# Stores off SyncE's queue, the last stage's first tile prepared during the second binary convolution, sums of y taken with VectorE's additions

## The chip, the cores and the metric

The kernel runs on one core of a Trainium2 chip. A core has five engines that run side by side, each with its own instruction stream in a fixed order: TensorE (PE, matrix products; PEld is its loading of weights), VectorE (DVE), ScalarE (ACT), GpSimd (POOL) and SyncE (SP, which here only starts DMA transfers). Any of ACT, POOL and SP can start a DMA; a transfer that waits for its data holds up what stands behind it in the same engine's stream. An engine waits for another by a semaphore. Data that is worked on lies in SBUF (128 partitions); PE writes to PSUM. The metric is the device time in microseconds (us).

## The reference

A tensor `x` of shape (4, 256, 64, 64), float32, goes through four residual layers, each `x = x + layer(group_norm(x))` with 32 groups of 8 channels. Layer 0 is an axial attention, layer 1 a 3x3 convolution with ternary weights, layer 2 a binary block and layer 3 a 3x3 convolution with a full set of weights. The change touches layers 1 to 3. Layer 2, cut to what matters (its input is the group norm of x):

```python
x = channel_shuffle(x, 2)
xa, xb = jnp.split(x, 2, axis=1)                      # 128 channels each
x1 = leaky_relu(gconv3x3(jnp.sign(x), w1, groups=2))  # 256 -> 128 channels
x2 = batchnorm_train(x1, g1, b1)                      # over batch and image
x3 = channel_shuffle(batchnorm_train(jnp.concatenate((x2 + xa, xb), 1), g2, b2), 2)
x4 = batchnorm_train(leaky_relu(gconv3x3(jnp.sign(x3), w2, groups=2)), g3, b3)
x5a, x5b = jnp.split(x3, 2, axis=1)
return jnp.concatenate((x4 + x5a, x5b), axis=1)
```

`batchnorm_train` needs mean and variance over all four images, so nothing after it can use its scale before the last image's convolution is through. Layer 3 needs, for each image, the group norm of `x + layer 2`, with statistics for each image and group of 8 channels. Of the 256 channels that layer 2 returns, the first 128 hold x4 and the other 128 (x5b) don't: for those, layer 3's input can be made without the last batch norm (the kernel's tile t = 1).

## The kernel before

The layers run as stages one after the other; after the attention (to about 1521 us of the profiled execution) come stage "d" (layer 1), the binary block "e" (layer 2) and stage "g" (layer 3). A scheduler puts the instructions of each engine into one fixed order by priority, mostly that of the program; `tc.high_priority()` raises what stands in it. Each stage's SBUF tiles come from pools laid one after another; the pools of the next stage lie over those of the one before, so a tile can be filled as soon as the old tile under it is done with.

*Stages "d" and "g"* share `conv_layer`. The channels are two halves t = 0 and 1 of 128. An image half tile (t, h) holds 32 rows. The convolution is made with a row transform: `input_rows` makes of the padded tile `pad` six combinations of rows (12 DVE operations, lines 970 to 986, result `dtr` or `gtr`), `output_rows` multiplies each of the six with three shifted weights for both t (36 products of 128x512, float32, each two records in the trace, line 998) and combines the six sums on ACT and DVE (lines 1016 to 1033) and adds them to x. That is one chunk (b, h, co): 4 images x 2 halves x 2 halves of output channels = 16 chunks. For the first chunk, products of one t are all issued ahead of those of the other (`order`, which is (1, 0) in stage g). `prepare(b, t)` loads a tile, adds up x and takes its statistics; `norm` gets group means with small matmuls (`pst`, lines 111 to 122) and rsqrt (ACT, line 102); `transform` writes the normalised tile into the pad (ACT, lines 1108 and 1112) and calls `input_rows`. `rest` interleaves the chunks of an image with `prepare`, `norm` and `transform` of the next. Results are stored by `finish_1` (`x2_d`, line 1184) and `finish_3` (`out`, line 1484), on SP. In the names of the trace digits are left out: `x_d` is `x2_d`, `u_d` is `u3_d`.

*Stage "e"* has two binary convolutions, each of 16 chunks (4 images, 4 quarters q) of 72 bf16 matmul records (line 1230). `prepare_1` loads x2 (line 1311), writes signs into `e_pad` (ACT, line 1322), and `binary_rows` makes `e_tr` (DVE, line 1220). `binary_conv` copies one of the four sums (ACT, line 1238), combines them (DVE, 1239 to 1242), applies the leaky relu (DVE, two additions of 512 columns, line 1245: the result is y, which stays in SBUF), and takes on ACT the sum (1247) and the sum of squares (1248) of y. `chunk_1` also takes the sum of y times x (DVE 1334 into `junk`, ACT 1337). After convolution 1 the statistics of the whole batch give scales. `prepare_2` scales x (ACT 1427), adds y (DVE 1431), stores the result z on SP (`z_d`, 1434) and takes its signs (ACT 1440). `chunk_2` overwrites y with the second convolution's result and stores it on SP after every second chunk (`y_d`, 1449). `sums_affine` (1285) turns the sums of the batch into the last batch norm's scale `sy2` and shift `cy2`.

*Stage "g"* then starts: it zeroes its pads on POOL, loads six weight tiles of 768 KB on SP (1068), and for t = 1 and then 0 prepares image 0. `load_3` loads 1 MB halves of x (1461), then in eighths of a tile parts of z and x2 (1468, 1469), added by DVE (1470), and for t = 0 y (`yq`, loaded at 1475, added at 1476 with scale `sy2`); the statistics are DVE's (1037). In program order all of this stands behind the second binary convolution and its sums. These lines set the order of stage g's start:

```python
        set_up()
        load_weights()
        for t in (1, 0):
            prepare(0, t)
            norm(0, slice(t, t + 1))
            transform(0, t, 0)
        for t in (1, 0):
            transform(0, t, 1)
        rest()
```

## Time and profile before

| | us |
|---|---|
| median of 3 runs | 2985.82 |
| lowest and highest | 2976.44, 2987.91 |
| the profiled execution's own time | 2981.28 |
| its span | 2979.5 |
| stage d, where PE is busy 480.43 of 481 | 1618 to 2099 |
| binary convolution 1 | 2105 to 2242 |
| statistics | 2242 to 2267.3 |
| binary convolution 2 | 2267.3 to 2415.5 |
| first matmul of stage g's convolution | 2460.76 |
| last one ends, about | 2971.4 |

Read it by stages: the busy shares of the whole span mix stages with different limits. From 2494 to the end of its matmuls stage g keeps PE busy without a gap, as stage d does; the idle stretches of PE lie at the borders of the binary block. The granted TensorE clock is 0.940 of full speed over the span and about 1.00 in stage g's convolution once it runs.

### The profile page before, as it was taken

The page shows a single profiled execution, that of the slowest core. Times are in us where ns is not written, and L with a number is a line of the kernel's source. Part 1 is how long each engine was busy: PE and PEld are TensorE (multiplying, and loading weights), DVE is VectorE, ACT ScalarE, POOL GpSimd, SP SyncE. Part 2 cuts the span into 40 slices and gives each one's busy share as a digit, 9 for nine tenths or more (in the row PEclk, how much of TensorE's full clock was granted, in tenths as well). Part 3 has the DMA queues.
Part 4 walks back from the last instruction along what each step waited for, and adds up shares of the span by engine and source line. Part 5 has one row for each costly group of instructions (what it writes and reads, how often), then busy time and mean ns, then how long its engine had stood idle before and what let it go on. Part 6 is the DMA issues. An engine that isn't in the chain of part 4 may idle for free. (4 is left out here: it accounts for less than half of the span.)

```text
span 2979.5 us, 77554 instructions
## 1 busy us (share of the span) xinstructions
PE 2605.9 (87%) x34248; PEld 1609.6 (54%) x34248; DVE 2066.4 (69%) x3555; ACT 1084.8 (36%) x2073; POOL 55.7 (2%) x119
## 2 busy tenths in 40 slices
PE   7999889899999778888845999999996848999998
PEld 4656556677767566667642444444453533444443
DVE  6555997666666466666667898884777859869553
ACT  4554444555545644555401011011468620101100
POOL 0000000000000100000000000000000000000000
PEclk9999999999999798999867999999997978999999
DMA  6867465555464777888654533413336544243201
GB/s 234 265 202 216 133 189 140 139 142 138 111 143 109 224 254 242 266 264 269 218 180 165 181 112 120 161 51 146 104 120 228 210 180 136 95 147 109 92 28 43
DMA packets 246807, 484.65 MB, mean 163 GB/s; under 512 B 28672, under 2 KB 128640, under 8 KB 220608
## 3 DMA queue, kind: packets, MB, share of 16 engines
q1 hardware_dynamic: 190080, 349.19, 35.1%
q10 hardware_dynamic: 53728, 117.46, 14.3%
q0 software_dynamic: 2656, 12.98, 1.2%
q8 instruction: 271, 4.44, 0.6%
q14 instruction: 72, 0.59, 0.1%
HBM read 283.20 MB, written 196.35 MB: 161 GB/s over the span
## 5 line engine op out<-in xcount | busy, mean ns | idle before, releaser
L998 PE MATMUL gc<-gtr,g_u 128*128 128x512 f32 x1152 | 501.3, 597 | 21.4 <-issue 13.0
L998 PE MATMUL dc<-dtr,d_u 128*128 128x512 f32 x1152 | 503.6, 598 | 17.1 <-DVE dtr L984 11.6
L478 DVE STREAM_TRANSPOSE t<-pd 128x1024 f32<-128x1024 f32 x256 | 304.1, 1227 | 114.7 <-PE pd L471 114.7
L998 PEld LDWEIGHTS gc<-gtr,g_u 128*128 128x128 f32 x1152 | 218.6, 191 | 296.3 <-issue 283.6
L998 PEld LDWEIGHTS dc<-dtr,d_u 128*128 128x128 f32 x1152 | 217.8, 191 | 288.8 <-issue 265.4
L471 PE MATMUL pd<-rm,qb 64*32 64x256 f32 x8192 | 285.0, 388 | 51.9 <-DVE t L478 42.7
L490 PEld LDWEIGHTS pq<-t,t 64*64 64x64 f32 x8192 | 261.7, 137 | 72.0 <-issue 46.9
L1230 PE MATMUL pc<-e_tr,e_k 128*64 128x512 bf16 x2304 | 266.1, 392 | 39.0 <-ACT pc_o L1238 20.2
L490 PE MATMUL pq<-t,t 64*64 64x64 f32 x8192 | 281.3, 221 | 16.1 <-issue 14.0
L494 ACT ACTIVATE o<-pq 128x512 f32<-128x512 f32 x256 | 152.4, 595 | 321.9 <-PE pq L490 321.9
L1230 PEld LDWEIGHTS <-e_k 128*64 128x64 bf16 x2304 | 154.2, 112 | 149.6 <-issue 51.0
L797 ACT ACTIVATE pt<-pt,sm 128x512 f32<-128x512 f32 x256 | 162.9, 709 | 188.5 <-DVE pt L767 151.6
L471 PEld LDWEIGHTS pd<-rm,qb 64*32 64x32 f32 x8192 | 156.4, 108 | 135.0 <-DVE t L478 59.9
L767 DVE TENSOR_TENSOR pt<-e_False,si_False 128x1024 f32<-128x1024 f32 x128 | 151.5, 1218 | 41.0 <-PE e_False L757 40.8
L499 ACT ACTIVATE pq<-pq 128x512 f32<-128x512 f32 x256 | 149.8, 585 | 3.9
L757 PE MATMUL e_False<-qc_False,rw 32*128 32x256 f32 x1024 | 126.3, 478 | 20.8 <-DVE pt L767 11.7
L1016 ACT COPY gc_c<-gc 128x512 f32<-128x512 f32 x32 | 18.6, 581 | 343.7 <-PE gc L998 343.7
L1016 ACT COPY dc_c<-dc 128x512 f32<-128x512 f32 x32 | 18.7, 584 | 329.0 <-PE dc L998 329.0
L279 PE MATMUL po<-xg,wt 128*128 128x512 f32 x256 | 123.6, 623 | 9.2 <-DVE st L286 7.6
L835 PE MATMUL pa_False<-pt,vb 128*32 128x64 f32 x4096 | 100.9, 239 | 28.5 <-issue 18.0
L859 PE MATMUL pe_False<-pt,ve 128*32 128x64 f32 x4096 | 92.1, 245 | 32.6 <-issue 24.5
L294 PE MATMUL pv<-wt,xg 128*128 128x256 f32 x512 | 120.6, 384 | 0.0
(383 smaller groups left out, 3406.1 us busy)
## 6 DMA issues: line engine op xcount, KB each, us to landing
si_False<-qk_d SPq DMA_DIRECT2D x64, 1024.0 KB
qk_d<-o ACTq DMA_DIRECT2D x124, 512.0 KB
x<-x_d SPq DMA_DIRECT2D x32, 1056.0 KB
a<-at_d SPq DMA_DIRECT2D x256, 128.0 KB
xa<-in_x SPq DMA_DIRECT2D x16, 1024.0 KB
vt_d<-vs ACTq DMA_DIRECT2D x32, 512.0 KB
q_d<-qs SPq DMA_DIRECT2D x64, 256.0 KB
qb<-q_d SPq DMA_DIRECT2D x128, 128.0 KB
```

The source lines that it names most:

```text
L279: nc.tensor.matmul(psf, lhsT=wt[:, t, bass.ts(o, P)], rhs=xg[:, t, :], start=(t == 0), stop=(t == 1))
L294: nc.tensor.matmul(pv[:, j, :], lhsT=xg[:, t, pix], rhs=wt[:, t, C : 2 * C], start=(t == 0), stop=(t == 1),)
L471: nc.tensor.matmul(pds[t][32 * c : 32 * c + 32, m].rearrange("p j k -> p (j k)"), lhsT=q[rows, 2 * (gp % 2) + g, a, 32 * nb : 32 * nb + 32 ...
L478: nc.vector.transpose(ts[t][:, :, 32 * jh : 32 * jh + 32].rearrange("p a j b -> p j a b"), pds[t].rearrange("p m j k -> p j m k"),)
L490: nc.tensor.matmul(ps[rows, m, :], lhsT=ts[1][rows, n // 2, :, n % 2], rhs=ts[0][rows, n // 2, :, n % 2], start=True, stop=True, tile_posi ...
L494: nc.scalar.activation(o[:, :, 8 * k : 8 * k + 8, :], ps.rearrange("p n (a b) -> p a n b", b=2), AF.Copy, accum_out=acc[:, 0, gp, col : co ...
L499: nc.scalar.activation(psf, psf, AF.Square, accum_out=acc[:, 1, gp, col : col + 1])
L757: nc.tensor.matmul(es[x_ // 2][:, x_ % 2, :, :, par], lhsT=rw[rows, 63 - i : 127 - i].rearrange("p j r -> p (j r)"), rhs=q[rows, :, par, k ...
L767: nc.vector.tensor_tensor(dst, e, src, ALU.add)
L797: nc.scalar.activation(s, s, AF.Exp, scale=s2q[:, gp : gp + 1])
L998: nc.tensor.matmul(ms[k], lhsT=u[:, t, dx, k, bass.ts(co, P)], rhs=vs[t][:, k, :, dx : dx + 64], start=(first and dx == 0), stop=(last and ...
L1230: nc.tensor.matmul(m[64 * g : 64 * g + 64], lhsT=parts[:, g, i, k, dx, :], rhs=vs[g][:, k, 8 * (q % 2) : 8 * (q % 2) + 8, dx : dx + 64], s ...
```

## The change

Five things are changed.

1. The stores of x2, z and out go from SP's queue to GpSimd's, those of y to ACT's. Stage g's weights are loaded on GpSimd's queue, in the order t = 1, then t = 0. The pads of "d" and "g" are zeroed on DVE.
2. The sum of y (line 1247) and that of y times x (1337) are no longer taken by ACT: the DVE operations that make y and `junk` carry an accumulating output (`accum_out`); the product with x becomes a `scalar_tensor_tensor`. ACT keeps the squares.
3. `prepare(0, 1)`, `norm` and `transform` of image 0's tile t = 1 are no longer behind the second binary convolution: they have a higher priority, and the pools of "e" and "g" are laid in another order, so that the tiles they need don't lie over tiles that are still in use. In the resulting order on DVE their operations stand among those of the second convolution's last nine chunks, and five of the eight additions of z and x2 for t = 0 stand there too. On PE the 18 products of t = 1 for the first chunk follow the last binary matmul directly, and the group means of t = 0 come after them.
4. For image 0 and t = 0 alone the statistics are made of sums: the addition of y on DVE has an accumulating output, and ACT squares the result with another; the squares are written over the `yq` tile, of which there are two.
5. `transform(0, t, 1)` is pinned to its place in program order. In the resulting order on DVE, 15 additions and statistics for image 1 stand between t = 0's additions and the end of its 12 transform rows.

The core of the diff (bookkeeping of arguments is left out):

```diff
-    def input_rows(v, pad):
+    def input_rows(v, pad, pinned):
...
         stt = nc.vector.scalar_tensor_tensor
-        stt(v[:, 5], d[2], -4.0, d[4], ALU.mult, ALU.add)
+        start = stt(v[:, 5], d[2], -4.0, d[4], ALU.mult, ALU.add)
+        if pinned:
+            tc.keep_in_program_order(start)
         stt(v[:, 0], d[1], -4.0, d[3], ALU.mult, ALU.add)
...
         xslots = {k: pool(ph, f"{name}_x{k}") for k in x_order}
+        if name == "g":
+            op = pool(ph, f"{name}_o", 2)
         wp = pool(ph, f"{name}_w")
-        op = pool(ph, f"{name}_o", 2)
+        if name == "d":
+            op = pool(ph, f"{name}_o", 2)
         tslots = {k: pool(ph, f"{name}_t{k}") for k in tr_order}
...
         def set_up():
             for h in range(2):
-                nc.gpsimd.memset(pads[h][:, 33 * h, :], 0.0)
-                nc.gpsimd.memset(pads[h][:, 1 - h : 34 - h, 0], 0.0)
-                nc.gpsimd.memset(pads[h][:, 1 - h : 34 - h, 65], 0.0)
-
-        def load_weights():
-            for t in first:
-                for dx in range(3):
-                    nc.sync.dma_start(out=u[:, t, dx], in_=weights[:, t, dx])
+                nc.vector.memset(pads[h][:, 33 * h, :], 0.0)
+                nc.vector.memset(pads[h][:, 1 - h : 34 - h, 0], 0.0)
+                nc.vector.memset(pads[h][:, 1 - h : 34 - h, 65], 0.0)
+        def load_weights(t, eng):
+            for dx in range(3):
+                eng.dma_start(out=u[:, t, dx], in_=weights[:, t, dx])
...
             st = sp.tile([P, NB, 6], F32, name=f"{name}st_{b}_{t}", tag=f"st{t}")
-            shifts[b, t] = load(b, t, place(b, t), ap_, st, sp, pst)
-            nc.vector.bn_aggr(mvs[b][:, t, :], st.rearrange("p k s -> p (k s)"))
+            shifts[b, t], done = load(b, t, place(b, t), ap_, st, mvs[b][:, t, :], sp, pst)
+            if not done:
+                nc.vector.bn_aggr(mvs[b][:, t, :], st.rearrange("p k s -> p (k s)"))
             if shifts[b, t] is not None:
...
-        def transform(b, t, h):
+        def transform(b, t, h, pinned=False):
...
             v = tslots[s].tile([P, 6, 8, 66], F32, name=f"{name}tr_{b}_{t}_{h}", tag="tr")
-            input_rows(v, pads[h])
+            input_rows(v, pads[h], pinned)
             vs[b, t, h] = v
...
             half_stats(st_x2[b, co], h, xh)
-            nc.sync.dma_start(out=x2_d[b][bass.ts(co, P), bass.ts(h, HW // 2)], in_=xh)
+            nc.gpsimd.dma_start(out=x2_d[b][bass.ts(co, P), bass.ts(h, HW // 2)], in_=xh)
             if h == 1:
...
             prepare(0, 0)
-        load_weights()
+        for t in range(2):
+            load_weights(t, nc.sync)
         norm(0, slice(0, 1))
...
-    def binary_conv(psp, lp, parts, vs, q, dst, st, name):
+    def binary_conv(psp, lp, parts, vs, q, dst, sums, squares, name):
...
         for r in range(2):
-            nc.vector.scalar_tensor_tensor(rows[:, r], o[:, r], 0.01, o[:, r], ALU.mult, ALU.max)
-        of = o.rearrange("p r q w -> p (r q w)")
-        nc.scalar.activation(of, dst, AF.Copy, accum_out=st[:, 0:1])
-        nc.scalar.activation(of, dst, AF.Square, accum_out=st[:, 1:2])
+            nc.vector.scalar_tensor_tensor(
+                rows[:, r], o[:, r], 0.01, o[:, r], ALU.mult, ALU.max, accum_out=sums[:, r : r + 1]
+            )
+        nc.scalar.activation(o.rearrange("p r q w -> p (r q w)"), dst, AF.Square, accum_out=squares)
...
         padp = pool(ph, "e_p")
+        jp = pool(ph, "e_j")
+        yp = pool(ph, "e_y")
         sp = pool(ph, "e_s")
-        yp = pool(ph, "e_y")
         lp = pool(ph, "e_l")
         wp2 = pool(ph, "e_w2")
-        tslots = {k: pool(ph, f"e_t{k}") for k in (0, 2, 3)}
+        tslots = {k: pool(ph, f"e_t{k}") for k in range(4)}
         wp1 = pool(ph, "e_w1")
-        tslots.update({k: pool(ph, f"e_t{k}") for k in (1, 4, 5)})
+        tslots.update({k: pool(ph, f"e_t{k}") for k in (4, 5)})
         padq = pool(ph, "e_q")
-        jp = pool(ph, "e_j")
         psb = pool(ph, "e_pst", 1, PSUM)
...
         nmr2 = small(keep, [P, B, 2])
-        st = [sp.tile([P, B, 4, 2], F32, name=f"st_y{i}") for i in range(2)]
-
-        def sums_affine(st, gamma, beta):
+        sums = [sp.tile([P, B, 4, 2], F32, name=f"sum_y{i}") for i in range(2)]
+        squares = [sp.tile([P, B, 4], F32, name=f"sq_y{i}") for i in range(2)]
+        def sums_affine(i, gamma, beta):
             tot = small(sp, [P, 2])
-            nc.vector.tensor_reduce(tot, st.rearrange("p b q k -> p k (b q)"), AX.X, ALU.add)
+            nc.vector.tensor_reduce(tot[:, 0:1], sums[i].rearrange("p b q r -> p (b q r)"), AX.X, ALU.add)
+            nc.vector.tensor_reduce(tot[:, 1:2], squares[i].rearrange("p b q -> p (b q)"), AX.X, ALU.add)
             mv = small(sp, [P, 2])
...
         def chunk_1(b, q, vs):
             dst = y[b][:, bass.ts(q, 1024)]
             junk = jp.tile([P, 1024], F32, name=f"junk_{b}_{q}", tag="junk")
-            nc.vector.tensor_tensor(
-                junk, dst, xa[b, h][:, r : r + 16, :].rearrange("p h w -> p (h w)"), ALU.mult
+            nc.vector.scalar_tensor_tensor(
+                junk, dst, 1.0, xa[b, h][:, r : r + 16, :].rearrange("p h w -> p (h w)"), ALU.mult, ALU.mult,
+                accum_out=cross[:, b, q : q + 1],
             )
-            nc.scalar.activation(junk, junk, AF.Copy, accum_out=cross[:, b, q : q + 1])
...
         my = small(sp, [P, B])
-        nc.vector.tensor_reduce(my, st[0][:, :, :, 0], AX.X, ALU.add)
+        nc.vector.tensor_reduce(my, sums[0].rearrange("p b q r -> p b (q r)"), AX.X, ALU.add)
...
                     )
-                    nc.sync.dma_start(out=z_d[b][:, bass.ts(h, HW // 2)], in_=xf[:, 64 * h : 64 * h + HW // 2])
+                    nc.gpsimd.dma_start(out=z_d[b][:, bass.ts(h, HW // 2)], in_=xf[:, 64 * h : 64 * h + HW // 2])
                 for g in range(2):
...
         def chunk_2(b, q, vs):
...
                 cols = bass.ts(q // 2, HW // 2)
-                nc.sync.dma_start(out=y_d[b][:, cols], in_=y[b][:, cols])
-
-        images(prepare_2, chunk_2, [prepare_2(0, h) for h in range(2)])
-        _, sy2, cy2 = sums_affine(st[1], vec[:, V_G3 : V_G3 + 1], vec[:, V_B3 : V_B3 + 1])
+                nc.scalar.dma_start(out=y_d[b][:, cols], in_=y[b][:, cols])
+        with tc.high_priority():
+            ready = [prepare_2(0, 0)]
+        ready.append(prepare_2(0, 1))
+        images(prepare_2, chunk_2, ready)
+        _, sy2, cy2 = sums_affine(1, vec[:, V_G3 : V_G3 + 1], vec[:, V_B3 : V_B3 + 1])
...
-        def load_3(b, t, xh, ap_, st, sp, pst):
+        def load_3(b, t, xh, ap_, st, mv, sp, pst):
+            first = b == t == 0
             for half in range(2):
...
                         nc.sync.dma_start(out=yq, in_=y_d[b][:, part])
-                        nc.vector.scalar_tensor_tensor(xt[:, cols], yq, sy2, xt[:, cols], ALU.mult, ALU.add)
-                half_stats(st, half, xt)
+                        if not first:
+                            nc.vector.scalar_tensor_tensor(xt[:, cols], yq, sy2, xt[:, cols], ALU.mult, ALU.add)
+                            continue
+                        k = 4 * half + q
+                        nc.vector.scalar_tensor_tensor(
+                            xt[:, cols], yq, sy2, xt[:, cols], ALU.mult, ALU.add, accum_out=st[:, k, 0:1]
+                        )
+                        nc.scalar.activation(yq, xt[:, cols], AF.Square, accum_out=st[:, k, 1:2])
+                if not first:
+                    half_stats(st, half, xt)
             if t == 1:
-                return sg[:, 1, 1, b : b + 1]
+                return sg[:, 1, 1, b : b + 1], False
+            if first:
+                nc.vector.tensor_reduce(mv, st[:, :, 0:2].rearrange("p k s -> p s k"), AX.X, ALU.add)
+                nc.vector.tensor_scalar(mv, mv, 1.0 / HW, None, ALU.mult)
+                m2 = small(sp, [P, 1])
+                nc.vector.tensor_tensor(m2, mv[:, 0:1], mv[:, 0:1], ALU.mult)
+                nc.vector.tensor_tensor(mv[:, 1:2], mv[:, 1:2], m2, ALU.subtract)
+                nc.vector.tensor_scalar(mv[:, 1:2], mv[:, 1:2], 0.0, None, ALU.max)
             nc.vector.tensor_tensor(shift_y[:, b : b + 1], sg[:, 0, 1, b : b + 1], cy2, ALU.add)
-            return shift_y[:, b : b + 1]
+            return shift_y[:, b : b + 1], first
         def finish_3(b, h, co, xh, sp, pst):
-            nc.sync.dma_start(out=out[b, bass.ts(co, P), bass.ts(h, HW // 2)], in_=xh)
+            nc.gpsimd.dma_start(out=out[b, bass.ts(co, P), bass.ts(h, HW // 2)], in_=xh)
         set_up, load_weights, prepare, norm, transform, rest, sp, pst = conv_layer(
-            "g", ph, u3_d, (0, 1, 2, 3, 4, 5), (0, 1, 2, 4, 3, 5), M_GRP, load_3,
+            "g", ph, u3_d, (0, 1, 2, 3, 4, 5), (2, 3, 4, 5, 0, 1), M_GRP, load_3,
             vec[:, V_L3B : V_L3B + 2], (1, 0), finish_3,
         )
-        set_up()
-        load_weights()
+        with tc.high_priority():
+            set_up()
+        prepare(0, 1)
+        load_weights(1, nc.gpsimd)
+        with tc.high_priority():
+            norm(0, slice(1, 2))
+            transform(0, 1, 0)
+        load_weights(0, nc.gpsimd)
+        prepare(0, 0)
+        norm(0, slice(0, 1))
+        transform(0, 0, 0)
         for t in (1, 0):
-            prepare(0, t)
-            norm(0, slice(t, t + 1))
-            transform(0, t, 0)
-        for t in (1, 0):
-            transform(0, t, 1)
+            transform(0, t, 1, True)
         rest()
```

## The prediction

> **What bounds the kernel now.** I read the page first (span, clock), then tables of engine busy time cut at the stage borders, then the chain of waits and the timeline around the borders. Columns of the next fence: stretch in us, its length, then busy time (and instructions) of PE, PEld, DVE, ACT, POOL, then granted PE clock, DMA share, GB/s.
>
> ```profile
> span 2979.5 us, 77554 instructions
> 1618.00:2099.00 481.00, 480.43 (x1138) 212.70 (x1139) 383.56 (x677) 57.43 (x68) 1.81 (x12) 0.99 0.36 121
> 2105.00:2242.00 137.00, 131.20 (x1158) 73.28 (x1158) 112.47 (x190) 86.85 (x117) 0.00 (x0) 0.98 0.38 127
> 2242.00:2267.30 25.30, 1.71 (x11) 1.50 (x10) 19.34 (x57) 17.58 (x20) 0.00 (x0) 0.55 0.31 120
> 2267.30:2345.00 77.70, 63.10 (x500) 35.27 (x502) 61.87 (x86) 76.02 (x58) 0.00 (x0) 0.90 0.68 250
> 2345.00:2415.50 70.50, 70.50 (x642) 45.55 (x639) 51.12 (x81) 30.72 (x51) 0.52 (x6) 0.99 0.41 150
> 2415.50:2494.20 78.70, 28.57 (x76) 13.34 (x72) 58.22 (x128) 12.39 (x15) 0.00 (x0) 0.67 0.57 200
> 2601.00:2971.40 370.40, 370.40 (x872) 163.42 (x871) 227.51 (x384) 33.67 (x42) 0.00 (x0) 1.00 0.23 83
> ```
>
> The ternary convolution (1618 to 2099) and the last stage after 2494 are bound by PE. Binary convolution 1 (2105 to 2242) nearly so. The statistics (2242 to 2267) leave PE idle. Binary convolution 2 is bound by ACT in its first 77.7 us (76.02 busy) and by PE in the rest. From 2415.5 to 2494.2 PE works 28.57 of 78.7 us. That hole is what the change is aimed at; its waits and timeline:
>
> ```profile
> PE pst L111 <- DVE sm L1086: 28.5, 1, 28.5
> PE pc L1230 <- ACT pc_o L1238: 20.2, 9, 4.5
> PE gc L998 <- issue: 13.0, 1, 13.0
> ...
> 2342.92 72.52 PE pc L1230 x648
> 2419.61 4.97 DMA y_d<-y
> 2424.66 13.72 DMA gx<-x_d
> ...
> 2448.91 2.11 ACT g_pad L1108
> ...
> 2460.76 16.80 PE L998 MATMUL gc<-gtr,g_u 128*128 128x512 f32 x32 [13.02 <-issue]
> 2487.43 6.00 PE L998 MATMUL gc<-gtr,g_u 128*128 128x512 f32 x10 [7.58 <-DVE gtr L977]
> ```
>
> After the last binary matmul (T0 = 2415.5) the last y store, the six weight loads and the first gx load go through SP one behind the other; gx is there at 2438.4. Then come its statistics, ACT's pad and DVE's 12 rows of the transform; PE starts the last convolution at 2460.76, 45.3 us after T0. One chunk of it takes 30.9 us (two ACT copies of the same place in neighbouring chunks of the ternary stage, at 2025.41 and 2056.31), 16 chunks 494.4; it ends at 2971.4, after 510.6. So 16.2 us go to a cold start (32 matmuls in 16.8 us where 0.429 each gives 13.7) and the waits up to 2494. The last store ends 8.1 us later.
>
> **The change, part by part.**
>
> *Stores of x2, z and out to GpSimd's queue, y to ACT's, pad memsets to DVE.* In the ternary stage PE is busy 480.43 of 481 us: nothing there moves the end (0; without that cover the 12 memsets are 12 x 0.16 = 2 us). The memsets of e_pad stand on POOL between stores of the ternary stage's last image; the ACT pass that fills the pads last ends 40 us before binary convolution 1, cover for a late one. z and x2 are read back a stage later. The weights (6 x 768 KB) now stand behind z's last store on POOL, about 80 us before T0 (the additions that make z end near 2330 to 2340); at the 5.4 us that a 768 KB load of POOL's queue takes (u_d<-u) even one at a time they are in after 33, if their place in SBUF is free, which no view shows. The eight y stores cost ACT their issue, 0.32 each as on SP: 2.6 us, from ACT time that the sums set free. The `out` stores hide under matmuls, save the last: 5.6 us now; 5.4 x 1024/768 = 7.2 by the POOL row. Term: +1.6, bounds 0 and +3.
>
> *Sums of y.* ACT loses 32 copies with sums (L1247: 1.055 + 0.187) and 16 over junk (L1337: 1.041 + 0.186): 39.7 us in convolution 1 with half of the former, 19.9 in convolution 2. DVE gets them as an accumulator on 64 additions of 512 columns and 16 of 1024: one accumulator read each. The only such addition in the trace is L456: 0.421 for 256 columns, read 0.084. L1245 without accumulator is 0.689 for 512. Both fit 0.155 + 1.04 ns a column, so the accumulator slows L456 by nothing but its read; but L456 has one operand in PSUM, L1245 both in SBUF. I take 0.084 a piece (bounds 0 and, if such an operation ran at half its rate and its read cost ACT's 0.187, 0.72 per 512 columns).
>
> [...]
>
> Convolution 1: 16 chunks x 72 matmuls at 0.1117 (72.52/648 = 0.1119) are 128.7 of 137 us. DVE goes to 112.47 + 48 x 0.084 = 116.5, still below; ACT to 47. Of the 8.3 us above full rate, the waits for ACT's copy L1238 (20.2 us over both convolutions) should go, not those for x. Term -4, bounds -8.3 and 0. Statistics: behind the last y ACT has L1247 (1.24) and L1337 (1.23) less, DVE three reads more: -2.2, bounds -2.5 and 0.
>
> *First tile of the last stage (t=1 of image 0) inside convolution 2.* Counted in the order of instructions: DVE gets in the last nine chunks 13 additions like L1470 (0.75), 8 statistics (0.69), 12 transform rows (0.64 from start to start), 6 memsets and some 15 small ones (0.16), and 18 accumulator reads: 9.8 + 5.5 + 7.7 + 3.4 + 1.5 = 27.9. Second part of convolution 2: DVE 51.1 + 27.9 = 79 in 70.5 us, so DVE becomes its bound: +8.5. First part: seven chunks without L1247 take 8.7 from ACT, which bound it: -8.7 (PE needs 56, DVE 62). Together about 0, bounds -8.7 and +12 (small waits: PE now has this tile's group sums between its matmuls and waits there for DVE, with chunks 15 and 16 queued behind them; ACT's norm and pad stand likewise ahead of the copy of the last chunk; a miss delays both convolutions' PE work by the miss). This tile's loads (two of gx, 16 of x) cost SP some 0.55 each, 10 us, in a stretch where DMA is busy to 0.41, and ACT's 5 us of pads lie where ACT is busy 30.7 of 70.5.
>
> *The hole.* t=1's products, half a chunk (15.5 us), follow T0 at once, PE warm. Then PE waits for t=0. Its chain from T0: output work and y 4.1, ACT's square 1.2, coefficients 2: sy2 at T0 + 7.5 (before: T0 + 9). Eight additions of y: two yq lie ready, and each further pair waits for addition (0.75), ACT's square of it (about 0.85), a load (2.6, the x load at 2439.69) and its turn: some 4.3 us a round, three rounds, so done at T0 + 23. Sums, group means and rsqrt 5 (2445.3 to 2448.9 plus additions), pad 2.1: T0 + 30. The transform shares DVE with additions for image 1 (15 such operations ordered among its 12 rows): its first rows at T0 + 33, all at T0 + 41; before, five such were among its 12 rows. PE takes the first two kinds of product (5.2 us) from T0 + 34 and goes on at T0 + 41, as if it had started at T0 + 36. Remaining 494.4 - 15.5 = 478.9, plus 3 cold: last matmul at T0 + 518 against T0 + 555.9. Term -38; bounds -48 (t=0 ready at T0 + 26, no cold loss) and -22 (t=0 another 16 later, by loads).
>
> Sum: 0 + 1.6 - 4 - 2.2 + 0 - 38 = -42.6. The profiled execution took 2981.28 (span 2979.5 and 1.8 around it): 2938.7. It lies 0.15% below the median 2985.82, within the spread of 11.5; I say 2939.
>
> **The rivals.**
>
> *A, the early tile is paid back.* DVE is in order, and at 79 of 70.5 us has no slack; a tile's load or a wait for PE's sums adds to it in full. Convolution 2 +12, t=0 at its late bound: 1.6 - 4 - 2.2 + 12 - 22 = -14.6: 2967. For it: DVE was 88% busy in the changed half; against: t=1's inputs are ready since convolution 1.
>
> *B, half rate for the accumulating additions* (0.53 per 512 columns): convolution 1 has 64 such pieces: 34 us on DVE's 116.5 make 150, +13 over 137; convolution 2 +17; last stage +4: 1.6 + 13 - 2.2 + 17 - 34 = -5: 2976. For: no row shows two SBUF operands with an accumulator; against: L456 loses nothing.
>
> *C, the slower side.* The same place, but an accumulating addition of two SBUF operands costs e = 0.9 per 512 columns (half rate, a read like ACT's, and its write waited out). DVE has 20 us of slack in convolution 1, none after: 64e - 20 + 32e + 8e over the -38.6 of the other terms; it decides from e = 0.56 on. At 0.9: +35, that is 3016. Only the missing row speaks for it.
>
> *D, better than forecast:* t=0 early and convolution 2 at full rate: about -60: 2921.
>
> **How the numbers follow.** Forecast 0.58, A 0.19, B 0.08, C 0.07, D 0.08. What this kernel's measurement tells from no change is about 0.5%, 15 us. A's 0.19 are split, by its nearness to that bound, into 0.10 faster, 0.07 same and 0.02 slower; B is same, C slower: faster 0.58 + 0.08 + 0.10 = 0.76, same 0.15, slower 0.09. The range: D's end at 2915, and A wholly inside, 2972; B and C are left out.
>
> **What would show it.** L1247 and L1337 gone; the additions at L1252 at 0.69 with reads of 0.08 (B and C: 1.2 or more). Convolution 2 still near 148 us, with DVE over 90% busy in its second half. PE's wait between t=1's and t=0's products about 20 us; first t=0 product at T0 + 34. The forecast is wrong if PE waits again for `g_u`, or if convolution 1 is longer than 137.

## The result, and the profile after

The changed kernel takes 2949.84 us (median of 16 runs, 2937.56 to 2976.9); the kernel before takes 2986.42 on the same chip (16 runs, 2976.44 to 3001.58). The ratio is 0.9884, 95% interval 0.986 to 0.9908: 36.6 us faster, less than the 42.6 forecast. The profiled execution of the changed kernel took 2953.15 us with a span of 2951.4.

The next fence is the table of busy time by stretch of the changed kernel, columns as in the prediction: binary convolution 1, the statistics, convolution 2 in two parts, and two pieces of what was the hole. Line numbers behind the change are higher: L1230 is now L1237, L1238 is L1245, L1245 is L1252, L998 is L1000, L1470 is L1484 and L1476 is L1494; in the experiments they move by a few lines more.

```profile
2111.46:2244.10 132.64, 128.36 (x1160) 68.94 (x1159) 113.61 (x236) 57.62 (x62) 0.53 (x1) 1.00 0.41 140
2244.10:2266.05 21.95, 1.53 (x8) 1.38 (x9) 18.59 (x62) 13.28 (x12) 1.54 (x3) 0.62 0.34 126
2266.05:2336.00 69.95, 68.57 (x596) 36.00 (x598) 64.79 (x108) 68.80 (x49) 2.19 (x5) 0.97 0.78 282
2336.00:2407.20 71.20, 65.42 (x566) 38.71 (x562) 57.36 (x118) 24.51 (x32) 3.74 (x7) 0.95 0.71 259
2407.20:2417.40 10.20, 0.00 (x0) 0.00 (x0) 10.20 (x20) 1.74 (x3) 0.00 (x0) 0.63 0.12 35
2432.80:2456.40 23.60, 7.61 (x14) 3.68 (x14) 15.51 (x42) 6.58 (x15) 0.00 (x0) 0.67 0.61 192
```

Convolution 1 is 4.4 us shorter and the statistics 3.1. Convolution 2 now holds the early tile's work and is still 9 us shorter (150.1 to 141.1). Its first half is filled by ACT (68.80 of 69.95 us busy) and PE (68.57) alike; in the second no engine is full: DVE is 57.36 of 71.20 us busy, where the forecast had it as the bound. Its last matmul ends at 2407.17, which is T0 from here on. (The prediction took 2415.5 as T0 of the kernel before; that kernel's last binary matmul ends at 2417.4. By that T0 its last product ends 554.0 us later, not 555.9.) For the first 10.2 us after T0 PE does nothing at all while DVE is busy throughout, and there is a second gap before the tile t=0. These are PE's waits from convolution 1 to the last stage's start:

```profile
PE pst L111 <- DVE sm L1092: 16.5, 2, 11.5
PE pc L1237 <- DVE e_tr L1227: 14.9, 1, 14.9
PE gc L1000 <- DVE pc_o L1249: 10.2, 1, 10.2
PE psg L1401 <- DVE sg L1403: 5.5, 1, 5.5
PE gc L1000 <- DVE gtr L979: 4.6, 1, 4.6
PE pc L1237 <- ACT pc_o L1245: 2.3, 4, 1.1
```

ACT's copy, which PE waited for longest in convolution 2 before, is nearly gone (2.3 us). The 16.5 us in the first line are two waits of PE's group mean matmuls (`pst`) for the sums that DVE makes for them ("group sums" below), one inside convolution 2, one in the hole. PE's timeline shows both in their places:

```profile
2390.20 0.59 PE L111 MATMUL pst<-sm,mt 128*128 128x1 f32 x2 [5.00 <-DVE sm L1092]
2390.71 1.49 PE L1237 MATMUL pc<-e_tr,e_k 128*64 128x512 bf16 x6
...
2394.69 12.48 PE L1237 MATMUL pc<-e_tr,e_k 128*64 128x512 bf16 x105
2417.40 15.32 PE L1000 MATMUL gc<-gtr,g_u 128*128 128x512 f32 x28 [10.23 <-DVE pc_o L1249]
2444.25 0.59 PE L111 MATMUL pst<-sm,mt 128*128 128x1 f32 x2 [11.53 <-DVE sm L1092]
...
2456.47 3.78 PE L1000 MATMUL gc<-gtr,g_u 128*128 128x512 f32 x4 [4.61 <-DVE gtr L979]
```

PE waits 5.00 us inside convolution 2 for the early tile's own statistics; the six matmuls behind the wait take 1.49 us, 0.25 each instead of 0.112. After T0 the early tile's first product starts 10.2 us late: it waits for DVE's combination of the last chunk (L1249). t=0's first product stands at T0 + 49.3 (2456.47), where the forecast had T0 + 34 (32.1 by the true T0). The change's additions with an accumulator, in the view of one line (minimum/median/maximum in ns):

```profile
L1252 DVE SCALAR_TENSOR_TENSOR y<-pc_o x64: 682/687/695, 2125.2 to 2417.9; 128x512 f32<-128x512 f32 x64
L1252 DVE DVE_READ_ACCUMULATOR y<-pc_o x64: 80/83/90, 2125.8 to 2418.5; 128x1 f32 x64
```

0.687 us against 0.689 without accumulator: no half rate, and no rival B or C. The last stage's additions of y, with an accumulator and two different SBUF sources (L1494), take 0.75 us, as those of z without one do (L1484).

| term | forecast | measured between the two profiles |
|---|---|---|
| attention and ternary convolution | 0 | +7.65, -1.3 |
| convolution 1 | -4 | -4.4 (137.0 to 132.6) |
| statistics | -2.2 | -3.1 (25.1 to 22.0) |
| convolution 2 | 0 | -9.0 (150.1 to 141.1) |
| hole (T0 to the last product) | -38 | -20.4 (554.0 to 533.6) |
| last store | +1.6 | +2.5 (8.1 to 10.6) |
| sum without attention | -42.6 | -35.7 |

The attention stage isn't touched. Its end (the first ternary matmul) lay between 1566.7 and 1586.1 us in the profiles of this study, so the 7.65 is the spread of that stage, and small differences have to be read from the other stages.

### The profile page after: what moved, and what is told of

The parts are those of the page before. It is cut to its first block, busy times and chain, and to the rows that moved or that the text cites. A ratio compares the mean times of both kernels' runs of the same rounds, so it can differ in the third digit from the quotient of the medians.

```text
span 2951.4 us, 77589 instructions
## 1 busy us (share of the span) xinstructions
PE 2599.9 (88%) x34248; PEld 1592.9 (54%) x34248; DVE 2063.2 (70%) x3653; ACT 1040.3 (35%) x1993; POOL 79.3 (3%) x153
## 3 DMA queue, kind: packets, MB, share of 16 engines
q10 hardware_dynamic: 54880, 125.84, 15.1%
## 5 line engine op out<-in xcount | busy, mean ns | idle before, releaser
L1000 PE MATMUL dc<-dtr,d_u 128*128 128x512 f32 x1152 | 504.2, 598 | 16.9 <-DVE dtr L986 11.5
L1000 PE MATMUL gc<-gtr,g_u 128*128 128x512 f32 x1152 | 505.2, 600 | 14.8 <-DVE pc_o L1249 10.2
L1000 PEld LDWEIGHTS gc<-gtr,g_u 128*128 128x128 f32 x1152 | 219.8, 192 | 291.4 <-issue 271.4
L1000 PEld LDWEIGHTS dc<-dtr,d_u 128*128 128x128 f32 x1152 | 218.1, 191 | 287.4 <-issue 264.6
L1237 PE MATMUL pc<-e_tr,e_k 128*64 128x512 bf16 x2304 | 260.0, 385 | 19.0 <-DVE e_tr L1227 14.9
L1237 PEld LDWEIGHTS <-e_k 128*64 128x64 bf16 x2304 | 141.2, 110 | 134.3 <-issue 21.5
L294 PE MATMUL pv<-wt,xg 128*128 128x256 f32 x512 | 122.2, 388 | 0.0
```

The lines of the kernel that those rows point to most:

```text
L294: nc.tensor.matmul(pv[:, j, :], lhsT=xg[:, t, pix], rhs=wt[:, t, C : 2 * C], start=(t == 0), stop=(t == 1),)
L1000: nc.tensor.matmul(ms[k], lhsT=u[:, t, dx, k, bass.ts(co, P)], rhs=vs[t][:, k, :, dx : dx + 64], start=(first and dx == 0), stop=(last and ...
L1237: nc.tensor.matmul(m[64 * g : 64 * g + 64], lhsT=parts[:, g, i, k, dx, :], rhs=vs[g][:, k, 8 * (q % 2) : 8 * (q % 2) + 8, dx : dx + 64], s ...
```

## The experiments

Every kernel below was timed beside the kernel before. Times are from each one's profile: convolution 1, statistics, convolution 2, T0 to the last product's end, from there to the span's end, and the sum of the last four. Convolution 1 stands apart because it moves by up to 5 us between kernels that have the same code there: 132.6 us at a granted clock of 1.00 in the changed kernel, 137.6 at 0.98 in e3. With the sums on DVE it is 134.3 on average (eleven profiles, 132.6 to 137.6), with them on ACT 138.3 (three, 137.0 to 139.2). The changed kernel profiled again (e6) repeats the sum within 0.3 us, but its convolution 2 is 1.7 us longer and T0 to the end 1.9 shorter: a difference of 2 us in one of these columns says nothing.

| kernel | conv 1 | stat. | conv 2 | T0 to end | tail | sum of 4 | median us, this / before | ratio (95%) |
|---|---|---|---|---|---|---|---|---|
| before | 137.0 | 25.1 | 150.1 | 554.0 | 8.1 | 737.3 | | |
| changed | 132.6 | 22.0 | 141.1 | 533.6 | 10.6 | 707.3 | 2949.84 / 2986.42 | 0.9884 (0.986 to 0.9908) |
| e1 queues | 138.8 | 25.2 | 152.3 | 545.4 | 10.6 | 733.5 | 2977.96 / 2979.42 | 0.9993 (0.997 to 1.0016) |
| e2 sums on ACT | 139.2 | 25.2 | 166.4 | 528.8 | 10.6 | 731.0 | 2974.68 / 2979.42 | 0.9984 (0.9962 to 1.0006) |
| e3 late tile | 137.6 | 22.0 | 130.9 | 541.6 | 10.6 | 705.1 | 2943.48 / 2979.42 | 0.9875 (0.9848 to 0.9902) |
| e4 yq ahead | 133.8 | 22.0 | 141.5 | 524.2 | 10.6 | 698.3 | 2933.39 / 2979.42 | 0.9852 (0.982 to 0.9885) |
| e5 sums only | 133.5 | 22.0 | 137.3 | 554.5 | 8.0 | 721.8 | 2962.15 / 2987.26 | 0.9909 (0.9876 to 0.9942) |
| e6 changed again | 132.8 | 22.0 | 142.8 | 531.7 | 10.5 | 707.0 | 2956.65 / 2987.26 | 0.9895 (0.9862 to 0.9928) |
| e7 rows behind | 136.4 | 22.0 | 141.9 | 524.6 | 10.6 | 699.1 | 2940.24 / 2987.26 | 0.984 (0.9806 to 0.9873) |
| e8 both | 133.1 | 22.0 | 139.8 | 522.5 | 10.6 | 694.9 | 2933.48 / 2987.26 | 0.9824 (0.9789 to 0.9858) |
| e9 means behind | 136.7 | 22.0 | 146.6 | 533.5 | 10.6 | 712.7 | 2950.1 / 2980.46 | 0.9888 (0.9859 to 0.9917) |
| e10 all | 134.2 | 22.0 | 136.6 | 520.5 | 7.3 | 686.4 | 2925.01 / 2980.46 | 0.9785 (0.9752 to 0.9818) |
| e11 all, t=0 early | 132.7 | 21.9 | 147.2 | 523.4 | 7.3 | 699.8 | 2933.79 / 2980.46 | 0.9846 (0.9807 to 0.9886) |
| e12 pieces | 134.3 | 22.0 | 141.7 | 531.0 | 10.6 | 705.2 | 2945.98 / 2980.76 | 0.9887 (0.9849 to 0.9925) |

**e1: the queues alone.** The kernel before with the stores moved (x2, z, `out` to GpSimd; y to ACT), the last stage's weights on GpSimd's queue and the pad memsets on DVE:

```
-                nc.sync.dma_start(out=y_d[b][:, cols], in_=y[b][:, cols])
+                nc.scalar.dma_start(out=y_d[b][:, cols], in_=y[b][:, cols])
...
-        load_weights()
+        load_weights(nc.gpsimd)
```

> The kernel before with part 1 of the change alone (x2, z and out on GpSimd's queue, y on ScalarE's, stage g's weights on GpSimd's, pads zeroed on VectorE). My account: it frees SyncE's queue, so that the first loads of the last stage no longer stand behind y's last stores and six weight loads (13 us of VectorE's idle time in the hole); in the resulting order half of tile t=1 is then added up during the second binary convolution. I expect the hole between the last binary matmul and the first product of stage g to fall from 45 us to some 30, and the time to some 2971 (-15). Rival: the queues alone are worth nothing (2986), all the gain comes from the early tile and the sums.

The ratio includes 1, as the rival had it, and the first product of `g` comes 37.5 us after T0, not 30. T0 to the end is 8.6 us shorter. That isn't because half of tile t=1 is added up during convolution 2: four of its eight additions stand there in the kernel before too, which its program order doesn't show. It is the wait for the rest of the tile. DVE's first such addition and its wait behind T0 in the kernel before, then the wait in e1:

```profile
2364.61 0.74 DVE L1470 SCALAR_TENSOR_TENSOR gx<-x,sg,gx 128x512 f32<-128x512 f32 x1
...
2438.41 1.41 DVE L1470 SCALAR_TENSOR_TENSOR gx<-x,sg,gx 128x512 f32<-128x512 f32 x2 [13.24 <-DMA gx<-x_d]
```

```profile
2433.81 1.42 DVE L1470 SCALAR_TENSOR_TENSOR gx<-x,sg,gx 128x512 f32<-128x512 f32 x2 [5.91 <-DMA gx<-x_d]
```

With y's stores and the six weight loads off SP, DVE's wait for the 1 MB load falls by 7.3 us (13.24 to 5.91). Convolutions 1 and 2 (+1.8, +2.2, within their spread) and the tail (+2.5) give most of it back.

**e2: the sums back on ACT, the rest as changed.** The second column of the sums is zeroed, as only one sum per chunk is left:

```
-                rows[:, r], o[:, r], 0.01, o[:, r], ALU.mult, ALU.max, accum_out=sums[:, r : r + 1]
...
+        nc.scalar.activation(of, dst, AF.Copy, accum_out=sums[:, 0:1])
```

> The changed kernel with the sums of y and of y times x back on ScalarE (part 2 undone). My account: the first convolution is 4 us longer, the statistics 3, the second convolution some 5 to 8 (ScalarE bounds its first half again): some 2963, 12 above the changed kernel. Rival (an accumulating addition costs VectorE what it saves ScalarE): no slower than the changed kernel, 2950 or less.

The whole gain goes: 23.7 us in the four stages, 6.6 in convolution 1, and the ratio includes 1 again. Convolution 2 is now 16.3 us longer than before the change. Its first part, and PE's waits from the statistics on:

```profile
2268.60:2352.00 83.40, 69.77 (x567) 37.48 (x569) 64.19 (x90) 80.86 (x63) 2.70 (x6) 0.91 0.70 256
```

```profile
PE pc L1237 <- ACT pc_o L1245: 17.5, 7, 6.0
...
PE pc L1237 <- DVE pc_o L1247: 7.7, 5, 2.7
```

ACT is 80.86 of 83.40 us busy, at PE's cost: 17.5 us of waits for its copy, and a clock of 0.91.

**e3: no early tile, all else as changed.** Both tiles of the last stage are held behind the first sum of convolution 2's statistics (the moved pools and the first binary tile's priority stay):

```
+        with tc.issue_after(stats_2.ins):
+            prepare(0, 1)
```

> The changed kernel with VectorE's operations for tile t=1 and t=0 of image 0 ordered behind the last convolution's sums, as they mostly stood before (queues, sums and pools as changed). My account: VectorE ends the second binary convolution some 7 us earlier against its matmuls, but the first product of stage g then waits for some 25 us of VectorE's work: stage g starts about 30 us after the last binary matmul, and t=0 is later too; time some 2962, 12 above the changed kernel. Rival: the early tile is paid back in full by VectorE in the second convolution: within 4 us of the changed kernel.

(e3 also holds back the four additions that the kernel before ran in convolution 2.) This is the run that decided most, and its rival held. It is no slower than the changed kernel: 705.1 against 707.3 us in the four stages, ratio 0.9875. The early tile brings its first product forward from T0 + 40.2 to T0 + 10.2, but the end only from T0 + 541.6 to T0 + 533.6, and convolution 2 pays 10.2 for it. The two halves of convolution 2 and PE's waits from there to T0 in e3:

```profile
2262.50:2328.00 65.50, 64.33 (x558) 33.36 (x559) 60.76 (x99) 64.41 (x46) 2.17 (x5) 0.97 0.81 279
2328.00:2393.40 65.40, 65.17 (x597) 41.67 (x593) 48.43 (x98) 25.77 (x33) 3.74 (x7) 1.00 0.66 255
```

```profile
...
PE pc L1237 <- ACT pc_o L1245: 0.7, 2, 0.5
PE pc L1237 <- DVE pc_o L1247: 0.6, 1, 0.6
```

Against them the kernel before, from the start of its convolution 2 (PE's waits, then three lines of its timeline):

```profile
PE pc L1230 <- ACT pc_o L1238: 14.6, 4, 4.5
```

```profile
2304.86 10.27 PE L1230 MATMUL pc<-e_tr,e_k 128*64 128x512 bf16 x72 [4.53 <-ACT pc_o L1238]
2317.92 8.04 PE L1230 MATMUL pc<-e_tr,e_k 128*64 128x512 bf16 x72 [2.79 <-ACT pc_o L1238]
2328.80 9.71 PE L1230 MATMUL pc<-e_tr,e_k 128*64 128x512 bf16 x72 [2.84 <-ACT pc_o L1238]
```

Without the early tile PE is busy in 129.5 of 130.9 us. Before, it lost 14.6 us in four waits for ACT, and behind two of them the next 72 matmuls took 10.27 and 9.71 us instead of the 8.04 of the line between. With what else e3 moves, convolution 2 is 19.2 us shorter than before (150.1 to 130.9), where the forecast counted only the 8.7 us of ACT's own removed copies.

**e5: the sums alone**, in the kernel before:

```
-        nc.scalar.activation(of, dst, AF.Copy, accum_out=st[:, 0:1])
...
+                rows[:, r], o[:, r], 0.01, o[:, r], ALU.mult, ALU.max, accum_out=sums[:, r : r + 1]
```

> The kernel before with part 2 of the change alone (sums of y and of y times x taken by VectorE's accumulating additions; queues, pools and the order of the last stage as before). New theory, from the run with ScalarE's sums put back: ScalarE's copies with sums held up both binary convolutions, and taking them away is nearly the whole gain: first convolution 137 to 133, statistics 25 to 22, second convolution 150 to some 131; the hole stays at 43 us; time 26 us under the kernel before. The forecast's own terms for the sums were worth 4 + 2.2 + 8.7 = 15 us. Rival: without the early stores' queues the second convolution stays slow: under 10 us gained.

15.5 us in the four stages (12.8 of it in convolution 2) and 3.5 in convolution 1; ratio 0.9909. The hole stays as it was (554.5). What e3 has beside the sums brings 16.7 on top of this (721.8 to 705.1): 6.4 in convolution 2 and 12.9 behind T0, less the tail's 2.6. That is the queues, worth 3.8 alone, but also the moved pools, the first binary tile's priority, and parts 4 and 5 of the change; no run has the sums with the queues alone, so how the 16.7 divides isn't shown. The whole gain is there without the early tile.

**e6: the changed kernel again**, beside e5, e7 and e8.

> The changed kernel once more, for a comparison on the same chip: 0.988 of the kernel before.

**Why t=0 comes late.** DVE's timeline of the changed kernel behind T0 (2407.17):

```profile
2414.21 0.68 DVE L1246 TENSOR_TENSOR pc_o<-pc,pc_o 128x512 f32<-128x512 f32 x1
...
2417.88 0.08 DVE L1252 DVE_READ_ACCUMULATOR y<-pc_o 128x1 f32 x1
2417.88 0.69 DVE L1252 SCALAR_TENSOR_TENSOR y<-pc_o 128x512 f32<-128x512 f32 x1
...
2422.27 0.75 DVE L1494 SCALAR_TENSOR_TENSOR gx<-yq,sm,gx 128x512 f32<-128x512 f32 x1
...
2430.37 1.42 DVE L1484 SCALAR_TENSOR_TENSOR gx<-x,sg,gx 128x512 f32<-128x512 f32 x2 [5.70 <-DMA gx<-x_d]
2431.70 0.75 DVE L1494 SCALAR_TENSOR_TENSOR gx<-yq,sm,gx 128x512 f32<-128x512 f32 x1
...
2436.12 0.75 DVE L1494 SCALAR_TENSOR_TENSOR gx<-yq,sm,gx 128x512 f32<-128x512 f32 x1 [2.99 <-DMA yq<-y_d]
...
2442.82 0.18 DVE L1503 TENSOR_REDUCE sm<-gst 128x2 f32<-128x16 f32 x1 [0.84 <-ACT yq L1497]
```

Three delays, counted from the true T0 (the forecast's times are 1.9 less there). DVE first runs rows of the early tile's transform; the last chunk's combination comes at 2414.21 and the last y at 2417.88, so sy2 is ready at T0 + 15.1, not 5.6: 9.5 late. In the second of the rounds of y's pieces DVE stands 5.70 us at an addition for image 1 (L1484) whose 1 MB load isn't there; two pieces of y lie behind it. With it the additions end at T0 + 34.7, not 21.1: another 4.1. From there to PE's first t=0 product it takes 14.6, not 11: 3.6. The sum, 17.2, is nearly the whole miss of that term (17.5: T0 + 533.6 against 516.1). It says where the time went, not what another order would save: see e7.

**e4: all of y's pieces loaded ahead.** Six of the eight go to a transform tile that is still free, instead of two buffers in turn:

```
+                        if first and k > 1:
+                            yq = spare[:, bass.ts(k - 2, HW // 8)]
```

> The changed kernel with six of the eight y pieces of image 0 loaded into a transform slot that is free (no longer two at a time behind ScalarE's squares). My account: the hole after t=1's products is set by the chain of t=0, 20 us of which are rounds of two y pieces each (4.4 us a round, the first 9.4); with the pieces there, the sums end some 12 us earlier and the time falls by 8 to 12, to some 2940. Rival: VectorE's order (image 1's additions ahead of t=0's rows) or the load of image 1 is the bound: less than 3 us.

T0 to the end is 9.4 us shorter (533.6 to 524.2; 7.5 against e6's 531.7), and the additions run without a gap (DVE's timeline, the first, the third and the last of the eight):

```profile
2413.61 0.75 DVE L1503 SCALAR_TENSOR_TENSOR gx<-yq,sm,gx 128x512 f32<-128x512 f32 x1
...
2415.02 0.75 DVE L1503 SCALAR_TENSOR_TENSOR gx<-yq_spare,sm,gx 128x512 f32<-128x512 f32 x1
...
2418.39 0.75 DVE L1503 SCALAR_TENSOR_TENSOR gx<-yq_spare,sm,gx 128x512 f32<-128x512 f32 x1
```

**e7: the early tile's rows and t=0's first additions behind the last y**, on top of e4; **e8: the same with the early tile's statistics from sums** (accumulators on its additions, squares on ACT):

```
+            with tc.issue_after(last_y[0]):
+                transform(0, 1, 0)
```

```
+                    kw = {"accum_out": st[:, k, 0:1]} if b == 0 and t == 1 else {}
...
+                        nc.scalar.activation(a, xt[:, cols], AF.Square, accum_out=st[:, k, 1:2])
```

> The kernel with y's pieces loaded ahead, and of the early tile only the additions, the statistics and the norm left inside the second convolution: t=1's 12 transform rows and t=0's additions of z are ordered behind the last y. Theory: in the changed kernel VectorE's early work makes the second convolution 10 us longer (131 to 141) and then holds up its last combination by 7 us; the 17 us that VectorE has free there hold the additions and statistics (12 us) but not rows and t=0 (13 more). Second convolution some 133, last matmul of the last stage some 522 us after it, time 10 under the kernel with y's pieces ahead. Rival: VectorE's total work up to t=0's sums is what counts, wherever it stands: within 3 us of that kernel.

> As the run before, and t=1's statistics taken from sums too (an accumulating addition on VectorE, squares on ScalarE) instead of eight statistics instructions of VectorE (0.69 us each). Theory (VectorE bounds the end of the second convolution): 2 to 5 us less than the run before. Rival: with rows and t=0 out of the way VectorE no longer bounds it: no difference.

e7 is a miss: convolution 2 stays at 141.9 us. DVE's load on its own there wasn't the cost. Its wait for loads fell from 12.6 to 5.2 us, but PE's 5.0 for the group sums stayed. Nor did T0 to the end gain (524.6 against e4's 524.2), though the last combination no longer stands behind the early tile's rows: now the rows stand behind it, and PE's first product comes 11.4 us after T0, as they end (9.9 in e4). e8 takes 2.1 off convolution 2 and 2.1 behind T0, no more than the spread between two profiles. e8, with the edits of e4 and e7 in it, is 23.2 us faster than the changed kernel on the same chip (2933.48 against 2956.65).

**What convolution 2 waits for.** DVE's longest waits in the second half of the changed kernel's convolution 2:

```profile
DVE gx L1484 <- DMA x<-x_d: 12.6, 4, 5.7
```

Two of the four waits are at pieces of the early tile (3.58 and 1.16 us), ahead of its group sums; the other two (2.13 and 5.68) are at t=0's pieces behind them. The load that the first one waits for took 8.46 us, as the chain of work that ended last shows it:

```profile
2361.11 8.46 DMA x<-x_d
```

The prediction had 2.6 us for a load of a piece of y. From the start of PE's wait (2385.2) to T0 are 22.0 us with 117 binary matmuls, which take 13.1 at 0.112 each. So 8.9 of the 10.2 us that the early tile costs convolution 2 stand at the group means: the wait, the small matmuls themselves and slower binary ones around them (the granted clock is 0.50 from 2390 to 2395).

**e9: PE's group means of the early tile behind chunk 15**, so that its own matmuls don't queue behind them:

```
+            with tc.issue_after(last_product["pc2_3_2"].ins):
+                norm(0, slice(1, 2))
```

> The changed kernel with one thing moved: TensorE's small matmuls for the group means of tile t=1 stand behind chunk 15 of the second convolution instead of in its midst. Theory, after the run with the rows moved left the second convolution at 142 us: its 10 us over 131 are TensorE's own wait for VectorE's sums at these matmuls (5.0 us in the trace) and the cold clock behind it, not VectorE's load. I expect the second convolution at 131 to 134 and the first product of stage g at most 8 us later after it; stage sum from the first matmul of the first convolution to the end 2 to 8 us under the changed kernel's 839.9. Rival (VectorE's load is the bound): the second convolution stays within 2 us of 141.

The idea that PE's place in the order alone was the cost fell: the wait moved and grew. PE's waits in e9 and two lines of its DVE's timeline:

```profile
PE pst L121 <- DVE sm L113: 10.8, 1, 10.8
```

```profile
2386.21 0.75 DVE L1486 SCALAR_TENSOR_TENSOR gx<-x,sg,gx 128x512 f32<-128x512 f32 x1 [5.99 <-DMA x<-x_d]
2388.20 0.15 DVE L113 TENSOR_TENSOR sm<-sm,pst 128x1 f32<-128x1 f32 x1
```

DVE stands 5.99 us at a piece of t=0's input that hasn't landed, and the one small operation PE needs (0.15 us) lies behind it. Convolution 2 is 146.6.

**e12: is it the two buffers or the transfers?** Six of the early tile's eight input pieces get places of their own:

```
+                    if b == 0 and t == 1 and k > 1:
+                        a = spare[:, bass.ts(k - 2, HW // 8)]
```

> The changed kernel with six of t=1's eight pieces of z and x2 loaded into a free transform slot instead of two buffers in turn. Theory, after the run with the norm moved made the second convolution longer (146.6): VectorE, in its fixed order, stands waiting for these pieces (12.6 us at the line of the addition in the second half), and TensorE for VectorE's norm; it is loads, not VectorE's or TensorE's work, that cost the 10 us. With the pieces loaded ahead VectorE's waits for them fall under 6 us and the second convolution to some 133 to 136. Rival: the queue is slow anyway (DMA is busy to 0.7 there): the waits move to other pieces and the second convolution stays within 3 us of 141.

DVE's waits, three lines of its timeline and a stretch of convolution 2 in e12:

```profile
DVE gx L1494 <- DMA x<-x_d: 10.3, 2, 6.4
```

```profile
2362.27 0.75 DVE L1494 SCALAR_TENSOR_TENSOR gx<-x,sg,gx 128x512 f32<-128x512 f32 x1 [3.94 <-DMA x<-x_d]
...
2367.21 1.41 DVE L1494 SCALAR_TENSOR_TENSOR gx<-x_spare,sg,gx 128x512 f32<-128x512 f32 x2
...
2394.06 0.75 DVE L1494 SCALAR_TENSOR_TENSOR gx<-x,sg,gx 128x512 f32<-128x512 f32 x1 [6.38 <-DMA x<-x_d]
```

```profile
2364.60:2400.00 35.40, 29.41 (x232) 15.35 (x228) 25.76 (x58) 10.05 (x14) 3.19 (x6) 0.90 0.79 294
```

The waits are still 10.3 us and convolution 2 141.7, so the rival held: they moved to other pieces. No addition of a piece with its own place (`x_spare`) waits; both waits are at pieces of t=0, which still take the two buffers in turn, and the first two of these now stand ahead of the six in the order. So e12 doesn't say what places for all pieces would bring. The loads that wait run in a stretch where DMA is 0.79 busy and moves 294 GB/s. Before the change the second half of convolution 2 had 0.41 and 150 GB/s; the prediction read its room for the early tile's loads from that. e3, with the tile held back, has 0.66 and 255 there, so more than its loads came in (the weights' six, now issued in convolution 2, are among them). No run moves these loads alone; that the busier queues make the pieces late is argued, not shown.

**e10: all of it**: e8, e9's edit, and the last image's stores back on SP; **e11: the same, but t=1's rows and t=0's additions early as in the change.**

```
+            eng = nc.sync if b == B - 1 else nc.gpsimd
```

> Everything together: y's pieces ahead, rows and t=0's additions behind the last y, t=1's statistics from sums, its group means behind chunk 15, and the last image's out stores back on SyncE's queue. Theory: second convolution 131 to 134 (from 139.8 in the run without the last two), the tail after the last product 8.0 instead of 10.6, the rest as there: stage sum 818 to 822 (from 828), time 0.979 of the kernel before. Rival for the tail: 10.6 as before, the queue makes no difference.

> As the run before, but rows and t=0's additions where the scheduler puts them (inside the second convolution). Theory: VectorE has room for them only in part; the last combination of the second convolution is late again and the second convolution 2 to 6 us longer, t=0's sums earlier by as much: within 4 us of the run before. Rival: VectorE's room suffices, 5 us or more under the run before.

PE's waits in e10 from convolution 2 on:

```profile
PE gc L1000 <- issue: 11.4, 1, 11.4
PE gc L1000 <- DVE gtr L979: 3.0, 1, 3.0
PE pst L111 <- DVE sm L1095: 2.0, 2, 1.3
PE pst L121 <- DVE sm L113: 1.8, 1, 1.8
```

No wait for group sums is over 2 us, convolution 2 is 136.6 (131 to 134 was expected) and the tail 7.3. e10 beats both kernels: 2925.01 us, ratio 0.9785 (0.9752 to 0.9818) against 0.9884 (0.986 to 0.9908) for the change. e11 puts 10.6 us back into convolution 2: DVE's waits for loads there rise from 8.6 to 18.3 us. So it is the combination that pays, not e9's edit. t=0's early additions cost nothing with PE's group means in their first place (141.1 in the changed kernel, 141.9 without them in e7), and some 10 us with the means behind chunk 15 (146.6 in e9 and 147.2 in e11, 136.6 without them in e10): there they stand ahead of what the means wait for. (e7 and e10 hold the tile's rows back too, but in e9 and e11 no row runs until the means are through.)

## Why the prediction was right, and where its steps failed

The total was right, a little too low (2939 for 2949.84), on two large terms that were both wrong and partly cancel: convolution 2 (0, measured -9.0) and the hole (-38, measured -20.4). That the number came so near is in part luck.

- **Queues.** The +1.6 for the last store was +2.5, inside its bounds; e10 shows it is the queue (7.3 on SP). Nothing of `g_u` is waited for, as forecast, though its loads were issued only 27 us before T0 (2380.4), not about 80.
- **Sums.** Right in kind: accumulator reads of 0.083 us that delay nothing, statistics -3.1 for -2.2, convolution 1 -4.4 for -4 (no larger than its spread in one pair of profiles, but -4.0 between the averages of all). The price of the additions, the point on which B and C hung, was right: the 64 of them take 0.687 us per 512 columns, no more than the 0.689 without accumulator. No run shows the half rate that the bound of 0.72, B's 0.53 (512 times 1.04 ns once more) and C's 0.9 us took, nor C's read of 0.187 or its wait for the write.
- **Convolution 2, ACT's relief.** The step "seven chunks without L1247 take 8.7 from ACT" was mis-sized: the relief is 12.8 (e5, the sums alone) and 19.2 with what e3 has beside them. The waits for ACT that went were worth more than the busy time that ACT lost: 14.6 us of waits became 0.7, and the slow matmuls behind two of them went too.
- **Convolution 2, the early tile.** The step "DVE 51.1 + 27.9 = 79 in 70.5 us, so DVE becomes its bound: +8.5" failed. The size was near (+10.2, from e3 to the change), the cause was not: DVE is 57.36 of 71.20 us busy in the second half, 81% and not the 90% that the prediction asked for, and over the whole convolution it does only 13.0 us more than in e3 (64.79 + 57.36 against 60.76 + 48.43); eight of the early tile's 12 transform rows run after T0. The 51.1 also held four additions and four statistics of this tile already (5.7 us), which the 27.9 counts again. What costs is PE standing at DVE's group sums, and DVE at loads ahead of them (4.7 us of waits there for PE's 5.0): the sentence given to rival A. e7 and e9 show that neither moving DVE's rows nor PE's order alone removes it; e10 removes about half.
- **The hole.** "Its chain from T0: output work and y 4.1 ..." failed by what stands ahead on DVE: t=1's rows before the last y (9.5) and image 1's addition (most of 4.1). The three rounds of 4.3 had no room for the second. "t=1's products follow T0 at once, PE warm" failed too: they start 10.2 us late, and 28 records take 15.32 us, 0.547 each where the prediction has 0.429, at a granted clock of 0.80 (2417.4 to 2432.8). -20.4 lies just outside the term's bounds (-48 to -22), and close to the -22 that rival A took.
- **Rival A** therefore held for the early tile's two prices, and only left out ACT's relief in convolution 2 (its sum was 2967). As it is, the early tile as placed is worth nothing (e3), and the gain is that of the sums and, only on top of them, of the rest that e3 keeps, the queues among it.

What stays open: why convolution 1 runs at a clock of 1.00 in some profiles and 0.97 or 0.98 in others, which of the parts that e3 keeps take the 6.4 us in convolution 2 and the 12.9 behind T0 that e5 still has (parts 4 and 5, the pools and the first binary tile's priority were never run alone), and what the 5.7 us are that e10's convolution 2 still has over e3's. Also open is whether the early tile pays anything in e10: e3 with e4's edit and the last stores on SP was not run. If both were worth there what they were on the changed kernel, its four stages would take 692.4 us (705.1 less 9.4 and 3.3, an estimate) against e10's 686.4.

## What to carry to other kernels

Price work moved onto an engine that runs in order by when the inputs of each instruction land and by what lies behind it, not by adding busy times: DVE had 19 us idle in the changed convolution 2 (141.1 less 122.2 busy), and PE still waited 5.0 us for it there; in e9 one operation of 0.15 us behind a late load held PE for 10.8. When a change has parts, run each alone and each left out: here the sums paid alone, the queues and what goes with them only on top of the sums, and the early tile, which looked largest, paid nothing. Putting one piece of an engine's work ahead of another gains nothing where the next engine needs both: in e7 the last combination came ahead of the early tile's rows, PE's first product came no earlier (11.4 us after T0 against e4's 9.9), and T0 to the end stayed (524.6 against 524.2).

## What the runs showed of the hardware that was not expected

- An accumulator read on DVE (0.083 us) is hidden: the next operation starts at the same time as the read (both at 2417.88), and additions with it follow one another every 0.61 us. ACT's read of the same kind took 0.187 in the kernel before.
- The last store took 2.5 us longer to the span's end from GpSimd's queue than from SyncE's (10.6 against 8.1 in the kernel before, and 7.3 in e10); the issue itself took 0.53 us there and 0.33 on SP's.
- A wait of PE can cost more than itself: after one of 5.0 us the next six matmuls took 0.25 us each, against 0.112, and after one of 2.84 us the next 72 took 9.71 us; yet after one of 2.79 us they took 8.04, as without a wait.
